# Attention with the mask ahead of the exponentials, row sums on ACT, and a re-planned order of the instructions

## The chip, the cores and the metric

The kernel runs on one core of a Trainium2 chip. The core has five engines with a queue each: PE (matrix multiply), DVE (vector), ACT (activation functions), POOL (GpSimd) and SP, which here only starts DMAs. Each queue is worked off in order, and engines wait for one another by semaphores. Times are device microseconds (us) of one execution; lower is better.

## The reference

One "macaron" layer on x of 8 x 512 tokens with 128 features, in float32: a mixture-of-experts feed-forward, windowed attention, and the same feed-forward again, each added to x. The part that the change touches is the attention:

```
scores = einsum(q, k) / sqrt(128)                 # per window of 128 tokens
_, top_idx = top_k(scores, 32)
masked = where(top 32 of the row, scores, -inf)
attn = softmax(masked - max(masked))
out = attn @ v; out = where(out >= 0, out, 0.01 * out)
x = x + layernorm(out + x_normed) * gamma + beta
```

Each row of 128 scores keeps its 32 largest, and the softmax goes over these alone. The feed-forward normalizes, routes each token to 2 of 8 experts (384 hidden features, SiLU gate times up, then down), weighs the two results, and adds a shared expert of 128 hidden features.

## The kernel before

The 8 batch entries are 8 blocks of 512 tokens; a block is a tile of 128 partitions by 4 windows by 128. Blocks 0 to 3 form group 0, blocks 4 to 7 group 1. The work runs group by group: first feed-forward (norm, routing, experts), attention, second feed-forward. The experts of one group are taken while the attention of the other is under way.

**Routing and experts.** `norm` (from line 532) normalizes a block, writes its rows to DRAM and makes the routing logits, which DVE copies out (`lgs`, line 568). When all four blocks of a group have theirs, `route` (from line 593) sorts the token-expert pairs on DVE, partly with PE; its result `src` (line 742) says which row goes where. Then POOL starts indirect gathers of 128 rows each (`xg`, line 846), PE transposes them (line 858), and 39 tiles of the group go through `pair`: two times three matmuls with the gate and up weights (`pg` and `pu`, line 924), SiLU on ACT (line 932), the product on DVE (`s`, line 935), three matmuls down (`y`, line 940), a copy on ACT (line 954), and an indirect write of the rows by POOL (line 962). The weights of a tile (`wt`) are copied by DVE (line 899) for two of the four runs of experts, and fetched by SP (line 901) for the others. At the end a block's rows are fetched back (`yg`) and added with their gates (line 999).

**Attention** (from line 1037) works on one block at a time: norm, transposes, q, k and v on PE, scores on PE, and a scaled copy of these by ACT into `sc` (line 1074). To find the 32 largest of a row, DVE runs four rounds: `max` gives the 8 largest (line 1084), and `match_replace` writes `tk`, a copy in which they are replaced by TAKEN, -3e38 (line 1088). Each is four instructions, one per window. The first of the maxima, negated, is `nm` (line 1092). `exps` (line 1099) takes exp(sc - max) of all 128 scores of a row on ACT, in place; it needs the first round alone. After the last round one DVE instruction (line 1103) keeps exp where `tk` is TAKEN and puts zero elsewhere. `sums` (lines 1107 and 1108) adds up each row and takes the reciprocal, `rs`. PE transposes the masked values (`pTp`, line 512), ACT copies them out (line 1113), PE multiplies with v (line 1118), and ACT scales each row by `rs` (line 1124). Then follow the leaky step, the residual on POOL, a norm and the sum into x, after which the block goes into the second `norm`.

ACT's Exp and Silu are in different tables; a load (ACT_TABLE_LOAD) comes in front of an activation whose table isn't there.

**The order.** The order of all instructions is worked out when the kernel is built. Each operation is entered in a plan with its engine, an assumed duration, what it reads and writes, and a due time. `schedule` then goes through time: of the operations that can start next on an engine it picks the one that is due first. Due times follow from constants: `PACE` is the spacing of the experts' tiles of the four runs; `LAG` is the spacing of the attention blocks of a group and `STRETCH` how due times grow along a block; `SHARED` sets start and spacing of the shared experts in the first feed-forward; `ROUTE_B` when the first routing of group 1 is due; `PAIRS` and `PUTS` when two parts of the routing are due against the rest; `FINISH` when the last sums of group 0 are due. The queues of SP and POOL are ordered by the same plan. Where the plan sees PE idle for over 0.75 us, it puts in matmuls of an identity whose result (`unread`, line 448) nobody reads; they keep PE busy.

Of the kernel before, what the change touches and what calls it, by code (L numbers as in the profile page):

```python
# [12 lines left out]
AF = mybir.ActivationFunctionType  # L13
ALU = mybir.AluOpType
AX = mybir.AxisListType

P = 128
H = 128
NB = 8
W = 4  # L20
# [7 lines left out]
TAKEN = -3.0e38  # L28
# [30 lines left out]

PACE = (1.79, 2.74, 2.27, 0.89)
LAG, STRETCH, ROUTE_STRETCH = 9.73, -0.34, 3.22
NORM_B, NORM_LAG, NORM_STRETCH = 7.11, 1.83, 1.14
SHARED = ((28.42, 6.74), (33.75, 24.46))
SHARED1 = ((114.02, 8.44), (5.88, 23.46))
ROUTE_B = 38.08
PAIRS, PUTS = 0.5, 4.89
FINISH = 18.87


class Buf:
# [180 lines left out]
def kernel(  # L253
# [16 lines left out]
    nc = tc.nc  # L270
# [32 lines left out]
    def act(us, fn, r, w, **k):  # L303
        return plan.op("ACT", us, fn, r, w, **k)

    def dve(us, fn, r, w, **k):
        return plan.op("DVE", us, fn, r, w, **k)
# [11 lines left out]
    def buf(shape, tag, name, dtype=F32):  # L319
        return Buf(sb, shape, tag, name, dtype)  # L320

    def bank(kind, name):
        return Buf(ps, [P, W, P], "ps", name, kind=f"ps_{kind}")
# [127 lines left out]
    def stats(src, r, name):  # L451

        st, mv = buf([P, W, 6], "st", f"st{name}"), buf([P, W, 2], "mv", f"mv{name}")

        def bn():
            for w in range(W):
                nc.vector.bn_stats(st()[:, w, :], src()[:, w, :])

        def aggr():
            for w in range(W):  # L460
                nc.vector.bn_aggr(mv()[:, w, :], st()[:, w, :])

        dve(0.87, bn, r, [st])
        dve(0.36, aggr, [st], [mv])
        return mv

    def scales(mv, name, eps):

        ve, rstd = buf([P, W], "ve", f"ve{name}"), buf([P, W], "rstd", f"rstd{name}")
        act(0.2, lambda: nc.scalar.activation(ve(), mv()[:, :, 1], AF.Identity, bias=eps),  # L470
            [mv], [ve], hold=[rstd])
        pool(1.05, lambda: nc.gpsimd.tensor_tensor(rstd(), ve(), mhalf, ALU.pow), [ve], [rstd])
        return rstd

    def shifts(mv, rstd, name):
        nb = buf([P, W], "nb", f"nb{name}")
        dve(
            0.16,
            lambda: nc.vector.scalar_tensor_tensor(  # L479
                nb(), mv()[:, :, 0], -1.0, rstd(), ALU.mult, ALU.mult  # L480
            ),
            [mv, rstd], [nb],
        )
        return nb
# [11 lines left out]
    def normalize_act(dst, src, r, rstd, nb):  # L496
        def run():
            for w in range(W):
                nc.scalar.activation(  # L499
                    dst()[:, w, :], src()[:, w, :], AF.Identity,  # L500
                    bias=nb()[:, w : w + 1], scale=rstd()[:, w : w + 1],
                )

        act(1.65, run, [*r, rstd, nb], [dst])
# [532 lines left out]
    def attention(b):  # L1037
        xk = ("x", b)
        ve, mm = nc.vector, nc.tensor.matmul
        h = buf([P, W, H], "h", f"ha_{b}")  # L1040
        mv = stats(lambda: xs[b], [xk], f"_a_{b}")
        rstd = scales(mv, f"_a_{b}", eps1)
        normalize_act(h, lambda: xs[b], [xk], rstd, shifts(mv, rstd, f"_a_{b}"))

        pool(1.27, lambda: nc.gpsimd.tensor_tensor(
            xs[b], xs[b], be_sb.to_broadcast([P, W, H]), ALU.add), [xk, "be"], [xk])
        hT = buf([P, W, P], "a0", f"haT_{b}")
        tp = transposed(h, [h], f"hTp_{b}", hold=[hT])
        act(0.58, lambda tp=tp: nc.scalar.copy(hT(), tp()), [tp], [hT])
        qk = []  # L1050
        for i, c in enumerate("qk"):
            pq, t = bank("m", f"p{c}_{b}"), buf([P, W, P], f"a{i + 1}", f"{c}T_{b}")
            pe(0.85, lambda pq=pq, i=i: mm(pq(), wqkv[:, i, :], hT(), start=True, stop=True),
               [hT, "wqkv"], [pq], hold=[t])
            act(0.68, lambda pq=pq, i=i, t=t: nc.scalar.activation(
                t(), pq(), AF.Identity, bias=bqk_sb[:, i : i + 1]), [pq, "bqk"], [t])
            qk.append(t)
        v, pv = buf([P, W, H], "v", f"v_{b}"), bank("m", f"pv_{b}")

        def values():  # L1060
            for w in range(W):
                mm(pv()[:, w, :], hT()[:, w, :], wqkv[:, 2, :], start=True, stop=True)  # L1062

        pe(0.9, values, [hT, "wqkv"], [pv], hold=[v])
        dve(0.69, lambda: ve.tensor_tensor(v(), pv(), bv_sb.to_broadcast([P, W, H]), ALU.add),
            [pv, "bv"], [v])
        sc, psc = buf([P, W, P], "sc", f"sc_{b}"), bank("m", f"psc_{b}")

        def scores():
            for w in range(W):  # L1070
                mm(psc()[:, w, :], qk[0]()[:, w, :], qk[1]()[:, w, :], start=True, stop=True)

        pe(0.88, scores, qk, [psc], hold=[sc])
        act(0.58, lambda: nc.scalar.activation(sc(), psc(), AF.Copy, scale=float(H) ** -0.5),
            [psc], [sc])

        tk, nm = buf([P, W, P], "a0", f"tk_{b}"), buf([P, W], "nm", f"nm_{b}")
        src = sc
        for r in range(TOPK // 8):
            m8 = buf([P, W, 8], "am8", f"am8_{b}_{r}")  # L1080

            def largest(src=src, m8=m8):
                for w in range(W):
                    ve.max(m8()[:, w, :], src()[:, w, :])

            def take(src=src, m8=m8):
                for w in range(W):
                    ve.match_replace(tk()[:, w, :], m8()[:, w, :], src()[:, w, :], TAKEN)  # L1088

            dve(0.87, largest, [src], [m8])  # L1090
            if r == 0:
                dve(0.17, lambda m8=m8: ve.tensor_scalar(
                    nm(), m8()[:, :, 0], -1.0, None, ALU.mult), [m8], [nm])
            dve(1.08, take, [src, m8], [tk])
            src = tk

        def exps():
            for w in range(W):
                nc.scalar.activation(sc()[:, w, :], sc()[:, w, :], AF.Exp, bias=nm()[:, w : w + 1])

        act(1.3, exps, [sc, nm], [sc], table="exp")
        rs = buf([P, W, 1], "rs", f"rs_{b}")
        dve(0.69, lambda: ve.scalar_tensor_tensor(
            sc(), tk(), TAKEN, sc(), ALU.is_equal, ALU.mult), [tk, sc], [sc])

        def sums():
            ve.tensor_reduce(rs()[:, :, 0], sc(), AX.X, ALU.add)
            ve.reciprocal(rs(), rs())

        dve(0.88, sums, [sc], [rs])  # L1110
        pT = buf([P, W, P], "a1", f"pT_{b}")
        tp = transposed(sc, [sc], f"pTp_{b}", hold=[pT])
        act(0.6, lambda: nc.scalar.copy(pT(), tp()), [tp], [pT])
        po, o = bank("m", f"po_{b}"), buf([P, W, H], "a2", f"o_{b}")

        def mix():
            for w in range(W):
                mm(po()[:, w, :], pT()[:, w, :], v()[:, w, :], start=True, stop=True)

        pe(0.88, mix, [pT, v], [po], hold=[o])  # L1120

        def scaled():
            for w in range(W):
                nc.scalar.activation(o()[:, w, :], po()[:, w, :], AF.Copy, scale=rs()[:, w, :])

        act(1.25, scaled, [po, rs], [o])
        dve(0.68, lambda: ve.scalar_tensor_tensor(o(), o(), NEG_SLOPE, o(), ALU.mult, ALU.max),
            [o], [o])
        pool(1.37, lambda: nc.gpsimd.tensor_tensor(o(), o(), h(), ALU.add), [o, h], [o])
        mv = stats(o, [o], f"_o_{b}")  # L1130
        rstd = scales(mv, f"_o_{b}", eps1)
        normalize_act(o, o, [o], rstd, shifts(mv, rstd, f"_o_{b}"))
        pool(1.27, lambda: nc.gpsimd.tensor_tensor(
            o(), o(), ga_sb.to_broadcast([P, W, H]), ALU.mult), [o, "ga"], [o])
        dve(0.69, lambda: ve.tensor_tensor(xs[b], xs[b], o(), ALU.add), [xk, o], [xk])
# [18 lines left out]
    for g in range(NG):  # L1154
# [4 lines left out]
        for i, b in enumerate(blocks(g)):  # L1159
            at(SHARED[g][0] + i * SHARED[g][1])  # L1160
            shared(0, b)
        at(ROUTE_B * g, 2.0 * g)
        route(0, g)
        at(0.0)
    for g in range(NG):
        experts(0, g, PACE[g])
    for g in range(NG):
# [17 lines left out]
        at(0.0)  # L1185
        experts(1, g, PACE[2 + g])
        diag = {b: weigh(b) for b in blocks(g) if b in LAST_ON_PE}
        for b in sorted(blocks(g), key=lambda b: b % 2):
            if g == 0:
                at(plan.ops[-1].due + FINISH, 2.0)  # L1190
            if b in diag:
# [42 lines left out]
```

## Time and profile before

| | |
|---|---|
| time, median of 3 runs | 530.48 us (529.94 to 531.19) |
| the profiled execution: its time, its span | 636.27 us, 634.6 us |
| granted PE clock, mean | 0.951 |
| PE busy | 532.1 us, 84% |
| DVE busy | 375.4 us, 59% |
| ACT busy | 274.7 us, 43% |
| POOL busy | 368.1 us, 58% |

The profiled execution is one execution, with the recorder on; durations come from it. A row of a group names line, engine, operation, what is written and read, the count, then busy us and mean ns of one, and after the second bar the idle time just ahead of them with what ended it. Busy time of PE is modelled, since matmuls are pipelined. The count of matmul records is twice the count of matmuls here: 156 tiles of three matmuls down are 936 records at line 940.

### The profile page before, as it was taken

How to read it: one execution, taken by the hardware profiler on the slowest of the kernel's cores; microseconds unless marked ns; L12 is line 12 of the kernel's file. 1: busy time of each engine (PE TensorE's matmuls, PEld its weight loads, DVE VectorE, ACT ScalarE, POOL GpSimd, SP SyncE). 2: the span in 40 equal slices, each digit the busy share in tenths (PEclk: the TensorE clock that was granted, in tenths of full speed). 3: DMA queues.
4: the chain of work that ended last, by engine and by line, in shares of the span. 5: the costliest groups of instructions: out<-in, count | busy, mean ns of one | idle time of the engine just before them, and what ended most of it. 6: DMA issues, size and time to landing. Idle time of an engine off the chain costs nothing.

```text
span 634.6 us, 13493 instructions
## 1 busy us (share of the span) xinstructions
PE 532.1 (84%) x4064; PEld 486.0 (77%) x4064; DVE 375.4 (59%) x1440; ACT 274.7 (43%) x588; POOL 368.1 (58%) x484
## 2 busy tenths in 40 slices
PE   4996778796894999989998999899988497679986
PEld 3875767685784978879977889889877387679976
DVE  6485634474330588897479899985685255234412
ACT  5713222221231369887540589886542022223320
POOL 6117454554565477768654788788356446555450
PEclk9998998989998899999999899999999698889999
DMA  7911010111133853445626535366642412111015
GB/s 218 327 61 52 30 38 30 38 31 33 30 109 108 267 156 92 146 140 167 216 89 210 153 116 157 106 183 187 196 151 83 129 58 73 42 34 34 27 38 199
DMA packets 39611, 72.27 MB, mean 114 GB/s; under 512 B 7604, under 2 KB 17848, under 8 KB 39544
## 3 DMA queue, kind: packets, MB, share of 16 engines
q1 hardware_dynamic: 29880, 51.73, 26.5%
q0 software_dynamic: 9088, 18.63, 9.4%
q10 hardware_dynamic: 576, 1.05, 0.4%
q8 instruction: 38, 0.62, 0.4%
q14 instruction: 29, 0.24, 0.1%
HBM read 54.86 MB, written 16.52 MB: 112 GB/s over the span
## 4 chain that ended last, share of the span: by engine, by line
PE 64%; DVE 14%; another core or an unknown queue 8%; ACT 6%; issue 5%; DMA 1%; POOL 1%; DVEq 0%; ACTq 0%
PE y L940 16%; PE pg L924 16%; PE pu L924 14%; DVE s L935 3%; PE ysh L588 2%; PE lg L563 2%; DVE wt L899 2%; PE pus L582 2%; PE xTp L858 2%; PE pgs L579 2%; PE unread L448 2%; ACT n L499 1%; DVE lanes L723 1%; PE pv L1062 1%
## 5 line engine op out<-in xcount | busy, mean ns | idle before, releaser
L962 POOL DMA_INDIRECT ys<-yb,dst x156 | 159.6, 1023 | 157.7 <-ACT yb L954 133.4
L940 PE MATMUL y<-ew,s 128*128 x936 | 140.7, 290 | 59.1 <-DVE s L935 43.5
L940 PEld LDWEIGHTS y<-ew,s 128*128 128x128 f32 x936 | 123.5, 201 | 71.9 <-DVE s L935 36.1
L846 POOL DMA_INDIRECT xg<-rows,src x128 | 126.9, 991 | 70.7 <-issue 34.4
L932 ACT ACTIVATE s<-pg 128x384 f32<-128x384 f32 x156 | 75.4, 490 | 184.6 <-PE pg L924 57.9
L924 PE MATMUL pg<-xT,wt 128*128 (+1 forms) x936 | 138.7, 286 | 13.8 <-issue 10.3
L924 PEld LDWEIGHTS pg<-xT,wt 128*128 128x128 f32 x936 | 123.2, 200 | 22.2 <-issue 17.0
L924 PE MATMUL pu<-xT,wt 128*128 (+1 forms) x936 | 134.6, 281 | 2.0 <-issue 1.0
L899 DVE COPY wt<-egu 128x768 f32 x78 | 45.8, 587 | 135.9 <-PE pu L924 64.0
L924 PEld LDWEIGHTS pu<-xT,wt 128*128 128x128 f32 x936 | 121.9, 198 | 3.2 <-issue 1.5
L935 DVE TENSOR_TENSOR s<-pu,s 128x384 f32<-128x384 f32 x156 | 84.9, 549 | 54.8 <-PE pu L924 19.4
L954 ACT COPY yb<-y 128x512 f32<-128x512 f32 (+1 forms) x60 | 26.0, 435 | 53.5 <-PE y L940 29.7
L999 DVE SCALAR_TENSOR_TENSOR x<-yg,gates,x 128x128 f32<-128x128 f32 x112 | 33.3, 361 | 10.9 <-DMA yg<-ys 10.9
L863 ACT ACTIVATE xT<-xTp,gb 128x512 f32<-128x512 f32 (+2 forms) x34 | 25.5, 754 | 27.3 <-PE xTp L858 19.1
L448 PEld LDWEIGHTS unread<-ident 128*128 128x128 f32 x264 | 31.0, 192 | 1.9 <-issue 1.9
L448 PE MATMUL unread<-ident 128*128 128x128 f32 x264 | 31.8, 275 | 0.0
L563 PEld LDWEIGHTS lg<-rwT,nT 128*128 128x128 f32 x128 | 22.1, 261 | 5.0 <-ACT nT L554 3.1
L1088 DVE MATCH_REPLACE8 tk<-am,tk 128x128 f32<-128x128 f32 x96 | 25.3, 273 | 0.0
L563 PE MATMUL lg<-rwT,nT 128*128 128x8 f32 x128 | 21.9, 302 | 2.9 <-ACT nT L554 2.3
L499 ACT ACTIVATE n<-x,nb,rstd 128x128 f32<-128x128 f32 x56 | 22.8, 484 | 3.3 <-DVE nb L479 3.0
L858 PE MATMUL xTp<-ident,xg 128*128 128x128 f32 x128 | 21.4, 290 | 2.7 <-issue 2.1
L581 ACT ACTIVATE ss<-pgs 128x512 f32<-128x512 f32 x16 | 9.6, 597 | 28.4 <-PE pgs L579 18.8
(177 smaller groups left out, 700.0 us busy)
## 6 DMA issues: line engine op xcount, KB each, us to landing
wt<-in_expert_gu SPq DMA_DIRECT2D x78, 384.0 KB
yg<-ys SPq DMA_DIRECT2D x28, 256.0 KB
rows<-n SPq DMA_DIRECT2D x16, 256.0 KB
egu<-in_expert_gu SPq DMA_DIRECT2D x8, 384.0 KB
ys<-yb,dst POOLq DMA_INDIRECT x156
x<-in_x SPq DMA_DIRECT2D x8, 256.0 KB
xg<-rows,src POOLq DMA_INDIRECT x128
out_x<-x SPq DMA_DIRECT2D x8, 256.0 KB
```

What stands on the lines that cost most here:

```text
L448: plan.idle = lambda: nc.tensor.matmul(unread, ident, ident, start=True, stop=True)
L499: nc.scalar.activation(dst()[:, w, :], src()[:, w, :], AF.Identity, bias=nb()[:, w : w + 1], scale=rstd()[:, w : w + 1],)
L563: nc.tensor.matmul(lg()[:, w, 0:NE], nT()[:, w, :], rwT, start=True, stop=True)
L846: nc.gpsimd.indirect_dma_start(xg()[:, j, :], None, r.rows, bass.IndirectOffsetOnAxis(ap=r.src()[:, t : t + 1], axis=0),)
L858: nc.tensor.transpose(tp()[:, w, :], xg()[:, w, :], ident)
L899: nc.vector.tensor_copy(to, egu[:, bass.ds(row, 2 * FF)])
L924: nc.tensor.matmul(p()[:, f, :], wt()[:, c * NF + f, :], xT[:, bass.ds(offs[1], P)], start=True, stop=True,)
L932: act(0.49, lambda: nc.scalar.activation(s(), pg()[:, 0:NF, :], AF.Silu), [pg], [s], table="silu")
L935: dve(0.56, lambda: nc.vector.tensor_tensor(s(), pu()[:, 0:NF, :], s(), ALU.mult), [pu, s], [s])
L940: nc.tensor.matmul(y()[:, j, :], s()[:, f, :], ew[:, bass.ds(offs[0] + f * H, H)], start=(f == 0), stop=(f == NF - 1),)
L962: ins = nc.gpsimd.indirect_dma_start(r.ys, bass.IndirectOffsetOnAxis(ap=r.dst()[:, t : t + 1], axis=0), yb()[:, i, :], None,).ins
L999: nc.vector.scalar_tensor_tensor(xs[b][:, w, :], yg[k]()[:, w, :], gates()[:, k, q : q + 1], xs[b][:, w, :], ALU.mult, ALU.add,)
```

## The change

In `attention` the mask moves ahead of the exponentials. It is now (tk - TAKEN) - sc: where an element was taken, tk is TAKEN, and the result is -sc; elsewhere it is about 3e38, since the score is lost in the rounding. The exponential takes this with scale -1 and the bias -max, so that a taken element gives exp(sc - max) and the others give 0. Its four instructions each also have ACT write the sum of the row into `rs`. The DVE instruction that added up the rows is gone, and the reciprocal stands alone. Nine constants of the plan have new values, so the whole list of instructions is ordered anew.

```diff
-PACE = (1.79, 2.74, 2.27, 0.89)
-LAG, STRETCH, ROUTE_STRETCH = 9.73, -0.34, 3.22
+PACE = (1.79, 2.74, 2.38, 0.89)
+LAG, STRETCH, ROUTE_STRETCH = 8.76, 0.02, 3.22
 NORM_B, NORM_LAG, NORM_STRETCH = 7.11, 1.83, 1.14
-SHARED = ((28.42, 6.74), (33.75, 24.46))
+SHARED = ((28.42, 4.89), (33.75, 22.74))
 SHARED1 = ((114.02, 8.44), (5.88, 23.46))
-ROUTE_B = 38.08
-PAIRS, PUTS = 0.5, 4.89
-FINISH = 18.87
+ROUTE_B = 33.77
+PAIRS, PUTS = 0.71, 4.31
+FINISH = 13.21
...
+        dve(0.69, lambda: ve.scalar_tensor_tensor(
+            sc(), tk(), TAKEN, sc(), ALU.subtract, ALU.subtract), [tk, sc], [sc])
+        rs = buf([P, W, 1], "rs", f"rs_{b}")
+
         def exps():
             for w in range(W):
-                nc.scalar.activation(sc()[:, w, :], sc()[:, w, :], AF.Exp, bias=nm()[:, w : w + 1])
-
-        act(1.3, exps, [sc, nm], [sc], table="exp")
-        rs = buf([P, W, 1], "rs", f"rs_{b}")
-        dve(0.69, lambda: ve.scalar_tensor_tensor(
-            sc(), tk(), TAKEN, sc(), ALU.is_equal, ALU.mult), [tk, sc], [sc])
-
-        def sums():
-            ve.tensor_reduce(rs()[:, :, 0], sc(), AX.X, ALU.add)
-            ve.reciprocal(rs(), rs())
-
-        dve(0.88, sums, [sc], [rs])
+                nc.scalar.activation(
+                    sc()[:, w, :], sc()[:, w, :], AF.Exp, bias=nm()[:, w : w + 1], scale=-1.0,
+                    accum_out=rs()[:, w, :])
+
+        act(1.3, exps, [sc, nm], [sc, rs], table="exp")
+        dve(0.2, lambda: ve.reciprocal(rs(), rs()), [rs], [rs])
```

The plan's assumed duration of the exponentials stays at 1.3 us; on DVE it books 0.2 us for the reciprocal where it booked 0.88 us for sum and reciprocal.

## The prediction

> **What bounds the kernel now.** I read the page first, then the busy time by stage, the groups of instructions, the chain of work that ended last, and the order of time of each engine around the attention blocks.
>
> ```profile
> span 634.6 us, 13493 instructions
> PE 532.1 (84%) x4064; PEld 486.0 (77%) x4064; DVE 375.4 (59%) x1440; ACT 274.7 (43%) x588; POOL 368.1 (58%) x484
> PE 64%; DVE 14%; another core or an unknown queue 8%; ACT 6%; issue 5%; DMA 1%; POOL 1%; DVEq 0%; ACTq 0%
> ```
>
> PE carries 64% of the chain, so over the whole run it is the bound. The attention blocks are another matter; by stage:
>
> ```profile
> 240.00:280.00 40.00, 35.68 (x286) 32.33 (x285) 36.38 (x184) 35.09 (x75) 30.32 (x31) 1.00 0.45 136
> 320.00:360.00 40.00, 37.23 (x288) 32.24 (x287) 34.52 (x137) 12.53 (x31) 22.01 (x26) 0.96 0.51 159
> 360.00:400.00 40.00, 37.60 (x290) 33.46 (x289) 38.72 (x195) 33.63 (x72) 32.58 (x36) 1.00 0.42 128
> ```
>
> The columns are PE, PEld, DVE, ACT, POOL. In the two attention stages PE, DVE and ACT are all near full: there is no slack engine to push work to. What the stage hands on is seen at its end, in the orders of time of DVE, PE and POOL (start, length, what, idle time before it):
>
> ```profile
> 286.38 0.27 DVE L1088 MATCH_REPLACE8 tk<-am,tk 128x128 f32<-128x128 f32 x1
> 287.25 0.68 DVE L1103 SCALAR_TENSOR_TENSOR sc<-tk,sc 128x512 f32<-128x512 f32 x1
> 315.35 0.19 DVE L568 COPY lgs<-lg 128x32 f32<-128x32 f32 x1 [0.50 <-PE lg L563]
> 339.50 0.19 DVE L742 SCALAR_TENSOR_TENSOR src<-signed 128x32 uint32<-128x32 f32 x1
> 340.36 6.64 PE L448 MATMUL unread<-ident 128*128 128x128 f32 x58
> 344.03 4.87 DMA xg<-rows,src
> 491.26 0.94 PE L924 MATMUL pg<-xT,wt 128*128 x6 [1.20 <-issue]
> ```
>
> Block 3 is the last of its group. From its last match (286.4) its mask, transposes, mix, second norm and logits run one after the other to 315.35; routing follows to 339.5, POOL's first gathers land at 348.9, and only then do the experts of the next group start. Meanwhile PE has run out of experts' tiles: it multiplies identities that nobody reads, 29 of them or 6.6 us at 340 alone. So the end of block 3, and not PE, sets when PE gets work again. The same happens to block 7, more mildly: PE does such fillers from 485.9, and real work starts at 491.26.
>
> **Profiled and timed.** The profiled execution took 636.27 us (span 634.6), 106 us over the median of 530.48. The chain books 8.2% of the span, 52 us, on an unknown queue and 4.7%, 30 us, on issue, and after long pauses three expert matmuls take 1.28 us instead of 0.67. These pauses lie mostly in the expert-only stages; I found none over 2 us in 222 to 315. So I take the attention rows as they stand and carry the difference to the median microsecond for microsecond: a sum of +x means 636.27+x there and 530.48+x timed.
>
> **The change, part by part.** The rows it touches:
>
> ```profile
> L1099 ACT ACT_TABLE_LOAD x8 | 10.3, 1283 | 0.5 <-DVE tk L1088 0.3
> L1099 ACT ACTIVATE sc<-sc,nm 128x128 f32<-128x128 f32 x32 | 10.2, 390 | 0.1
> L1103 DVE SCALAR_TENSOR_TENSOR sc<-tk,sc 128x512 f32<-128x512 f32 x8 | 6.3, 789 | 0.0
> L1107 DVE TENSOR_REDUCE rs<-sc 128x4 f32<-128x512 f32 x8 | 5.3, 665 | 0.0
> L1108 DVE RECIPROCAL rs<-rs 128x4 f32<-128x4 f32 x8 | 1.4, 178 | 0.3
> L639 ACT ACTIVATE th<-th 128x16 f32<-128x16 f32 x4 | 0.8, 212 | 2.6 <-DVE th L638 2.6
> ```
>
> *Removed.* Eight row sums L1107 on DVE, 8 x 0.665 = 5.3 us of DVE in all. On the path to block 3's end lie at most those of blocks 0, 1 and 2 (its own comes behind its mask): 3 x 0.67 = 2.0 us if DVE were the bound throughout. It isn't: between the takes DVE stands idle 1.55 us at 251 and 1.65 us at 264, waiting for PE, and the chain runs over DVE only from 266 to 284, with one L1107 in it. So the gain is 0.67 to 2.0; I take 1.3.
>
> *Same instructions.* The mask stays one instruction of two inputs and the same size: 0.68 for 0.68. Its maximum of 1.58 us was one case beside POOL's addition at 243.2, which other neighbours could repeat or spare: -0.9 to +0.9, taken as 0. Scaling by -1 costs nothing, since the activation has its scale anyway. The reciprocal keeps its 0.18.
>
> *Moved.* Today the exponentials of a block need only the first take; ACT does them while DVE runs the three other rounds (block 3: load at 278.64, exponentials 279.94 to 281.2, mask at 287.25). Afterwards they need the mask, which needs the last take. That cover, some 6 us of DVE work, is gone, and the transposes of the probabilities wait for ACT instead of DVE. On the path come 4 exponentials, 1.28 us as a group (four of 0.39 that overlap), and the table load in front of them, 1.28 us, since the load itself waited on DVE in one of eight cases and would do so always when placed behind the wait. One more hand-over between engines: 0.1 us, from gaps of 0.02 to 0.3. If the exponentials of two blocks become neighbours, or the load is issued ahead, 1.28 goes away; so the term is 1.4 to 2.7, and I take 2.7. The step issues no DMA and passes nothing on SP's or POOL's queue.
>
> Here the Trainium skill speaks against the change more strongly: "ScalarE: Activation LUTs", section "What ACT_TABLE_LOAD costs", books 1.28 us for the load and another 1.38 us of draining for each switch. The row shows 1283 ns, and at 278.64 the exponentials begin 1.30 us after the load does, with the load itself 0.02 us behind its predecessor. By the rule block 3 would pay 4.0 instead of 2.7; I go by the row.
>
> *Added.* ACT's sums: no row shows an activation with such an output. The skill's "VectorE: DVE Perf Modes", section "Two Vector instructions with no wait between them", says that on DVE such an instruction is two, the second one reading the accumulator; if ACT does likewise, four reads a block follow. Bounds: nothing, or 4 x 0.21 (the smallest ACT row, L639) = 0.85 us a block, 6.8 us of ACT in all. I take 0.2 each, 0.8 a block, nearer to that row than to nothing, because the sum of each partition has to be written out by something.
>
> *A new wait.* The reciprocal on DVE now waits for ACT, where it followed DVE's own sum. Behind it in DVE's queue stand the next block's takes and the products L935, on which PE's y waits. If the list expects the exponentials 0.8 us early, DVE loses up to that in each of eight blocks, 3 of them ahead of a group's last. I take 0.2 on the path, bounds 0 and 2.4.
>
> *The order.* Later blocks of attention come due earlier (LAG 9.73 to 8.76: 1, 1.9 and 2.9 us for the second to fourth), so PE prefers them to tiles more often. At most the 3.2 us that DVE waited for PE come back, at worst as much is lost elsewhere, since all other due times of shared experts, routing and combining move too and with them SP's weight loads and POOL's gathers and puts: -2.9 to +2.9. I take -0.7, about one matmul group of 0.67 that a later block no longer waits for.
>
> *Sum on block 3's path:* 2.7 + 0.8 + 0.2 - 1.3 - 0.7 = +1.7 us. It lands in full, because it lengthens a stretch in which PE does fillers. For block 7 the same terms hold. The two don't add: attention of the second group starts from the writes of the first experts, which end about 331, and not from the routing of block 3; so the last experts start about 1.7 us later, once. The timed forecast is 530.48 + 1.7 = 532.2, in the profiled execution's own terms 638.0.
>
> **The rivals.** *Faster: DVE's relief and the order win.* If DVE is the bound throughout, all 2.0 come back, and if the order returns 2.9 while the table load leaves the path: 1.4 + 0.8 - 2.0 - 2.9 = -2.7, or 527.8. For it: DVE at 38.72 of 40 us. Against it: DVE waits for PE between takes, and block 3's end is a chain with no room. It decides from the point where block 3's logits come earlier than 28.9 us behind its last match plus what DVE gained. *Slower by more: ACT becomes the bound.* ACT is at 35.09 of 40 us; 0.8 a block in a full queue and exponentials queued behind other blocks' norms (1.65 us) give 2.7 + 0.8 + 1.65 + 1.5 for the DVE wait - 1.3 = +5.4, or 535.9. *No change to be measured:* PE fills the longer chain with tiles that the order kept back, or the accumulator is free and relief full: 2.7 - 2.0 - 0.7 = 0, or 530.5.
>
> **How the numbers follow.** A measurement here tells about 0.2%, 1.1 us, from no change. Likeliest case (531.6 to 534.5) 0.42; ACT as the bound 0.20; no change 0.11; faster 0.27. This gives slower 0.62, same 0.11, faster 0.27. The range reaches from 526.0, a little below the faster rival, for bounds of the order, to 537.5, for bounds of the waits.
>
> **What the new profile would show.** L1107 gone and about 0.67 less DVE per block; the exponentials behind the last match, with an ACT table load between mask and exponentials; from block 3's last match to its logits 32 us instead of 28.9; small ACT instructions of some 0.2 us between the exponentials; longer fillers ahead of the second routing's gathers. The prediction is wrong if that stretch has no fillers any more, if the order starts block 3 over 3 us sooner, or if the opening stage (PE fillers at 37 to 43), whose due times change too, moves by itself.

## The result, and the profile after

The changed kernel takes 536.13 us (median of 5 runs, 535.89 to 538.61); the kernel before, 530.77 us beside it (529.94 to 532.55). The ratio is 1.0114, 95% interval 1.0083 to 1.0146: slower, by 5.4 us. The forecast was 532.2 with a range of 526.0 to 537.5, and slower was the likeliest outcome at 0.62. So direction and range hold. The size does not: +1.7 was forecast, and the time is that of the rival in which ACT becomes the bound (535.9). In the experiments further down the runs of one kernel spread by up to 3%; times there are medians of all runs, while ratios and their intervals compare the fast runs alone (within 1.5% of the fastest), so that the two need not agree.

From the page of the changed kernel: the span, busy time of the engines, and the chain by engine.

```profile
span 536.9 us, 13595 instructions
PE 505.5 (94%) x4106; PEld 469.9 (88%) x4106; DVE 370.2 (69%) x1432; ACT 278.8 (52%) x620; POOL 369.9 (69%) x486
PE 62%; DVE 11%; ACT 9%; DMA 9%; POOL 3%; issue 3%; SPq 1%; ACTq 0%; DVEq 0%; POOLq 0%
```

DVE's busy time fell by 5.2 us, as the removed row sums say; ACT's rose by 4.1. ACT's share of the chain went from 6% to 9%, and DVE's from 14% to 11%. This execution took 538.61 us, the slowest of the five, 0.5% over the median. The profile of before had 636.27; its "unknown queue" of 8% is absent here. More on that below.

Busy time in 40 us of group 0's attention (PE, PEld, DVE, ACT, POOL):

```profile
200.00:240.00 40.00, 38.33 (x301) 34.57 (x300) 33.16 (x171) 38.41 (x97) 30.87 (x34) 1.00 0.50 154
```

Before, ACT had 35.09 of 40 us there, and DVE 36.38. The two have changed places: ACT 38.41, DVE 33.16. The windows are not the same work to the instruction, so this is a hint only.

The groups of instructions that the change touches:

```profile
L1104 ACT ACTIVATE sc<-sc,nm 128x128 f32<-128x128 f32 x32 | 12.4, 390 | 0.1
L1104 ACT ACT_TABLE_LOAD x8 | 10.3, 1283 | 0.1
L1104 ACT ACTIVATION_READ_ACCUMULATOR sc<-sc,nm 128x1 f32 x32 | 6.0, 187 | 0.0
L1109 DVE RECIPROCAL rs<-rs 128x4 f32<-128x4 f32 x8 | 1.3, 162 | 0.6 <-ACT sc L1104 0.6
L448 PE MATMUL unread<-ident 128*128 128x128 f32 x306 | 36.5, 275 | 0.0
```

The accumulator is indeed an instruction of its own on ACT, 187 ns. Table loads are 8, as before. PE does 153 fillers (306 records) where it did 132 (264 records, 31.8 us in all): the 42 added records are all of PE's 42 more (4106 for 4064). The orders of time of DVE, ACT and PE around block 3, the last of group 0, and up to the second routing:

```profile
228.08 0.27 DVE L1088 MATCH_REPLACE8 tk<-am,tk 128x128 f32<-128x128 f32 x1
229.58 0.68 DVE L1098 SCALAR_TENSOR_TENSOR sc<-tk,sc 128x512 f32<-128x512 f32 x1
229.93 1.64 ACT L499 ACTIVATE n<-x,nb,rstd 128x128 f32<-128x128 f32 x4
231.47 0.28 ACT L470 ACTIVATE ve_o<-mv_o,eps 128x4 f32<-128x4 f32 x1
231.77 1.28 ACT L1104 ACT_TABLE_LOAD   x1
233.07 0.40 ACT L1104 ACTIVATE sc<-sc,nm 128x128 f32<-128x128 f32 x1
...
234.62 0.76 ACT L554 ACTIVATE nT<-nTp,gb 128x512 f32<-128x512 f32 x1
235.29 1.64 ACT L499 ACTIVATE o<-o,nb_o,rstd_o 128x128 f32<-128x128 f32 x4
236.82 0.57 ACT L1112 COPY pT<-pTp 128x512 f32<-128x512 f32 x1
...
237.89 1.28 ACT L932 ACT_TABLE_LOAD   x1
...
239.57 1.14 ACT L1123 ACTIVATE o<-po,rs 128x128 f32<-128x128 f32 x4
...
261.80 0.19 DVE L568 COPY lgs<-lg 128x32 f32<-128x32 f32 x1 [0.84 <-PE lg L563]
...
279.57 3.51 PE L448 MATMUL unread<-ident 128*128 128x128 f32 x30
...
284.25 8.51 PE L448 MATMUL unread<-ident 128*128 128x128 f32 x74
```

And the same two steps of ACT in the kernel before (its mask ran 287.25 to 287.93):

```profile
289.37 0.58 ACT L1113 COPY pT<-pTp 128x512 f32<-128x512 f32 x1
291.30 1.14 ACT L1124 ACTIVATE o<-po,rs 128x128 f32<-128x128 f32 x4 [0.36 <-PE po L1118]
```

From the last match to the scaling of the output it is 11.49 us now (228.08 to 239.57), and was 4.92 (286.38 to 291.30). The difference of 6.57 splits, step by step, into: mask begun later behind the match, 1.50 for 0.87, +0.63; exponentials after the mask's end, +2.81, of which 1.51 stand behind another block's norm and `ve_o` and 1.30 behind the table load; the exponentials with their reads, 233.07 to 234.72, +1.65; from there to the copy of the probabilities 2.10 for 1.44, +0.66; from the copy to the scaling 2.75 for 1.93, +0.82. The copy waits for nothing that PE does: PE's four transposes began at 234.47 and took 0.63. It stands in ACT's queue behind `nT` and a norm. The scaling likewise stands behind a copy, Silu's table load and a Silu. By the logits, 1.8 us of the 6.57 are made up: last match to logits is 33.7 us for 29.0, where 32 had been forecast.

Block 7, the last of group 1, pays more. Its last match and the scaling of its output, first now, then before:

```profile
358.64 0.27 DVE L1088 MATCH_REPLACE8 tk<-am,tk 128x128 f32<-128x128 f32 x1
371.65 1.12 ACT L1123 ACTIVATE o<-po,rs 128x128 f32<-128x128 f32 x4
416.15 0.27 DVE L1088 MATCH_REPLACE8 tk<-am,tk 128x128 f32<-128x128 f32 x1
421.26 1.14 ACT L1124 ACTIVATE o<-po,rs 128x128 f32<-128x128 f32 x4 [0.65 <-PE po L1118]
```

That is 13.01 us for 5.11, and up to the logits 37.3 (395.96) for 31.1 (447.22): +6.2, against +4.7 at block 3.

The fillers tell what idle time of PE the plan foresaw while it waits for the second routings and their gathers. The kernel before has, behind block 3, the 58 records at 340.36 and two batches ahead of them; behind block 7 it has 6, 8 and 6 from 485.88 on:

```profile
334.16 2.84 PE L448 MATMUL unread<-ident 128*128 128x128 f32 x24
337.88 0.69 PE L448 MATMUL unread<-ident 128*128 128x128 f32 x4
487.89 1.06 PE L448 MATMUL unread<-ident 128*128 128x128 f32 x8
```

The changed kernel has the 30 and 74 shown above behind block 3, and 22, 18 and 6 from 425.80 on behind block 7:

```profile
425.80 2.62 PE L448 MATMUL unread<-ident 128*128 128x128 f32 x22
429.18 2.17 PE L448 MATMUL unread<-ident 128*128 128x128 f32 x18
```

So behind block 3 fillers went from 43 to 52 (10.2 to 12.0 us, +1.9), behind block 7 from 10 to 23 (2.7 to 5.6 us, +2.9). Their number is set by the list, whatever the chip; it is no measured wait.

The chain of work that ended last, in order of time (start, length, what), in the attention of group 0 and at block 7:

```profile
201.05 1.28 ACT L1104
202.34 1.65 ACT sc L1104 x8
...
206.02 1.27 ACT L932
...
214.56 1.58 ACT sc L1104 x8
...
217.36 1.28 ACT L932
...
231.77 1.28 ACT L1104
233.07 1.65 ACT sc L1104 x8
...
361.93 1.28 ACT L1104
...
363.54 1.34 ACT sc L1104 x7
...
365.75 1.28 ACT L932
```

The pieces at L1104 alone are the load of the exponentials' table, `sc` with them the exponentials, and those at L932 alone the load of Silu's table that has to follow. The chain runs through the exponentials of blocks 1, 2 and 3, and again of block 7. In group 0 these lines add up to 10.0 us (two loads, three sets of exponentials, two loads back). In the chain of the kernel before, the same stretch holds no exponential at all and one table load; of the moved work only a mask is in it:

```profile
242.84 1.28 ACT L932
272.32 0.59 DVE sc L1103
```

In group 1 the chain of the kernel before does hold exponentials with their loads, those of blocks 4 and 6:

```profile
368.25 1.28 ACT L1099
369.55 1.28 ACT sc L1099 x4
...
393.51 1.28 ACT L1099
...
395.11 0.97 ACT sc L1099 x3
```

So in group 0 the exponentials are new on the chain; in group 1 they moved on it, from blocks 4 and 6 to block 7, and the chain alone shows no growth there. Behind block 3's exponentials the chain goes on over PE's queue of experts (from 237.45), as it did before (from 284.43). The tail and PE's own work end close to each other: DVE is done with the counts for the routing at 275.1, and PE's queue comes to their matmuls (`rank`, line 664) at 275.84; before, it was 328.1 and 329.26.

### The profile page after: what moved, and what is told of

The parts are those of the page before. It is cut to its first block, busy times and chain, and to the rows that moved or that the text cites. A ratio compares the mean times of both kernels' runs of the same rounds, so it can differ in the third digit from the quotient of the medians.

```text
span 536.9 us, 13595 instructions
## 1 busy us (share of the span) xinstructions
PE 505.5 (94%) x4106; PEld 469.9 (88%) x4106; DVE 370.2 (69%) x1432; ACT 278.8 (52%) x620; POOL 369.9 (69%) x486
## 4 chain that ended last, share of the span: by engine, by line
PE 62%; DVE 11%; ACT 9%; DMA 9%; POOL 3%; issue 3%; SPq 1%; ACTq 0%; DVEq 0%; POOLq 0%
PE pg L924 16%; PE pu L924 15%; PE y L940 15%; DMA xg<-rows,src 3%; DVE tk L1088 3%; PE pgs L579 3%; DVE am L1084 2%; DMA wt<-in_expert_gu 2%; PE lg L563 2%; PE pus L582 2%; PE ysh L588 2%; PE xTp L858 2%; ACT n L499 2%; POOL xg L846 2%; DMA ys<-yb,dst 1%
## 5 line engine op out<-in xcount | busy, mean ns | idle before, releaser
L846 POOL DMA_INDIRECT xg<-rows,src x128 | 128.4, 1003 | 71.8 <-issue 32.1
L924 PE MATMUL pg<-xT,wt 128*128 (+1 forms) x936 | 133.2, 279 | 8.3 <-DMA wt<-in_expert_gu 2.5
L932 ACT ACTIVATE s<-pg 128x384 f32<-128x384 f32 x156 | 76.2, 491 | 113.1 <-PE pg L924 108.6
L924 PEld LDWEIGHTS pg<-xT,wt 128*128 128x128 f32 x936 | 118.5, 193 | 16.3 <-issue 8.2
L940 PE MATMUL y<-ew,s 128*128 x936 | 130.4, 276 | 1.7 <-ACT yb L954 1.0
L924 PE MATMUL pu<-xT,wt 128*128 (+1 forms) x936 | 131.4, 277 | 0.0
L940 PEld LDWEIGHTS y<-ew,s 128*128 128x128 f32 x936 | 117.1, 192 | 6.4 <-issue 3.2
L924 PEld LDWEIGHTS pu<-xT,wt 128*128 128x128 f32 x936 | 117.7, 193 | 0.7 <-issue 0.5
L899 DVE COPY wt<-egu 128x768 f32 x78 | 44.6, 571 | 57.0 <-PE pu L924 56.0
L448 PEld LDWEIGHTS unread<-ident 128*128 128x128 f32 x306 | 35.7, 192 | 2.0 <-issue 2.0
L448 PE MATMUL unread<-ident 128*128 128x128 f32 x306 | 36.5, 275 | 0.0
```

What stands on the lines that cost most here:

```text
L448: plan.idle = lambda: nc.tensor.matmul(unread, ident, ident, start=True, stop=True)
L846: nc.gpsimd.indirect_dma_start(xg()[:, j, :], None, r.rows, bass.IndirectOffsetOnAxis(ap=r.src()[:, t : t + 1], axis=0),)
L899: nc.vector.tensor_copy(to, egu[:, bass.ds(row, 2 * FF)])
L924: nc.tensor.matmul(p()[:, f, :], wt()[:, c * NF + f, :], xT[:, bass.ds(offs[1], P)], start=True, stop=True,)
L932: act(0.49, lambda: nc.scalar.activation(s(), pg()[:, 0:NF, :], AF.Silu), [pg], [s], table="silu")
L940: nc.tensor.matmul(y()[:, j, :], s()[:, f, :], ew[:, bass.ds(offs[0] + f * H, H)], start=(f == 0), stop=(f == NF - 1),)
```

## The experiments

The theory (A): behind the mask, the exponentials come onto the path that sets a group's end; this costs more than DVE's relief returns, and the new list of instructions wins part of it back. Rivals: (B) the sums on ACT are what costs; (C) the new list itself is the loss and the edit is harmless; (D) DVE's relief is worth far more or less than 1.3 us.

On the chips of these runs the kernel before itself takes 644 to 663 us. In its three profiles PE, DVE and ACT stand still together for up to 8 us at a time, in gaps over 0.3 us 44 to 51 us in all (4 us in the profile of the changed kernel above), and the mean granted clock of its runs is 0.92 to 0.96 (0.996 to 0.999 in the five runs of the changed kernel above); the rest of the difference was not looked into. Ratios are therefore taken on one chip alone, and stages against a trace of before from the same chip. "Stage" below is the time from the first maximum of a group's first block to the logits of its last. In three traces of before from these chips it is 84.9, 87.0 and 83.7 us for group 0 (83.6 in the profile shown before) and 82.2, 88.9 and 83.0 for group 1 (81.6).

**The kernel before, once on each of three chips**, for its traces.

> The kernel before, unchanged, for a second profiled execution, since the first one was 106 us longer than the timed runs. Both theories: about 530.5 us; if the pauses of the first profile belong to that execution alone, the span now is near 529 us, and the attention rows are as in the first profile: 28.9 us from block 3's last match to its logits. If the pauses belong to the kernel, the span is again well over 600 us.

> The kernel before, unchanged, once more. If its pauses depend on the chip that it runs on, about 530.5 us and a span near 529 with no pause over 2 us; if they come with any profile, again some 640 us. Attention rows as in the first two profiles: about 29 us from block 3's last match to its logits, 84 to 85 us from block 0's first maxima to block 3's logits.

> The kernel before, for a profile beside the kernel after on the same chip. Where the chip shows the pauses of the first profile, 640 to 670 us; where it doesn't, about 530.5 us, and then from block 0's first maxima to block 3's logits 82 to 84 us.

Measured in that one profiled execution: 644.73, 667.32 and 647.83 us. Block 3's tail, last match to logits, is 29.2, 29.6 and 29.0 us against 29.0 in the profile before, so this stretch lies outside the pauses. Block 7's is 31.3, 35.5 and 31.0 us against 31.1. In the third trace such a pause ends at 565.54: PE waits 4.22 us for DVE, which in turn stands 6.17 us on something that the profile can't name, and the first three matmuls afterwards take twice as long (1.65 us for 0.83).

**The edit alone, in the list of before** (every other instruction stays where it was):

```diff
-                nc.scalar.activation(sc()[:, w, :], sc()[:, w, :], AF.Exp, bias=nm()[:, w : w + 1])
+                nc.scalar.activation(
+                    sc()[:, w, :], sc()[:, w, :], AF.Exp, bias=nm()[:, w : w + 1], scale=-1.0,
+                    accum_out=rs()[:, w, :])
...
-        act(1.3, exps, [sc, nm], [sc], table="exp")
-        dve(0.69, lambda: ve.scalar_tensor_tensor(
-            sc(), tk(), TAKEN, sc(), ALU.is_equal, ALU.mult), [tk, sc], [sc])
+        act(1.3, lambda: None, [sc, nm], [sc], table="exp")
...
+        def mask():
+            ve.scalar_tensor_tensor(sc(), tk(), TAKEN, sc(), ALU.subtract, ALU.subtract)
+            exps()
...
-        dve(0.88, sums, [sc], [rs])
+        dve(0.69, mask, [tk, sc], [sc])
+        dve(0.88, lambda: ve.reciprocal(rs(), rs()), [sc], [rs])
```

The plan still sees the exponentials where they were, but nothing is issued there; they are issued behind the mask.

> The instructions of the kernel after, placed in the list of the kernel before: exponentials with their sums right behind the mask, the reciprocal where sum and reciprocal stood, every other instruction in its old place. Theory A (the exponentials on the path of blocks 3 and 7 are the cause): 533 to 537 us, with 3 to 4 us more from block 3's last match to its logits. Theory B (the new order is the cause, the edit itself costs nothing or gains): 529 to 531 us.

Measured: 665.17 against 647.95 us, ratio 1.0392 [1.0235, 1.0549]; theory A's 533 to 537 us would be 1.004 to 1.012, so it is far too low. The stages are 92.7 and 94.4 us, +7.8 and +12.2 on the same chip's trace of before. The group of the reciprocals in this kernel:

```profile
L1112 DVE RECIPROCAL rs<-rs 128x4 f32<-128x4 f32 x8 | 1.4, 178 | 13.1 <-ACT sc L1101 13.1
```

And its order of time of ACT at block 3, where the mask runs from 293.74 to 294.42:

```profile
291.83 1.28 ACT L1101 ACT_TABLE_LOAD   x1
294.46 0.40 ACT L1101 ACTIVATE sc<-sc,nm 128x128 f32<-128x128 f32 x1 [1.34 <-DVE sc L1108]
...
297.67 1.28 ACT L932 ACT_TABLE_LOAD   x1
...
299.35 0.58 ACT L1115 COPY pT<-pTp 128x512 f32<-128x512 f32 x1
```

The tail of block 3 is 32.7 us, +3.5, as theory A had it; that of block 7 is 37.3, +6.0. The rest of group 0's +7.8 arises ahead of block 3's tail; the wait of the reciprocal, 13.1 us over eight blocks, stops all of DVE behind it and fits that. And the table load is issued ahead of the wait: here it is over before the mask begins, and the exponentials start as the mask ends. In its place Silu's load now stands between them and the copy of the probabilities. So in this list the edit is not harmless. The list was not made for it, though: the total holds what its stopped queues cost, and is no price of the edit in a list of its own.

**The instructions of before, in the list of after** (exponentials issued right behind the first take, sum back on DVE ahead of the reciprocal):

```diff
-            dve(1.08, take, [src, m8], [tk])
+            if r == 0:
+                def take_and_exps(take=take):
+                    take()
+                    for w in range(W):
+                        nc.scalar.activation(
+                            sc()[:, w, :], sc()[:, w, :], AF.Exp, bias=nm()[:, w : w + 1])
+
+                dve(1.08, take_and_exps, [src, m8], [tk])
+            else:
+                dve(1.08, take, [src, m8], [tk])
...
+        act(1.3, lambda: None, [sc, nm], [sc, rs], table="exp")
...
-        dve(0.88, sums, [sc], [rs])
+        dve(0.2, sums, [rs], [rs])
```

> The reverse: the list of the kernel after, but with exponentials behind the first take, the mask behind the last one and the row sum on DVE, as in the kernel before. Theory A: 2 to 4 us faster than the kernel after, so 532 to 534 us. Theory B: as slow as the kernel after, 535.5 to 537 us.

Measured: 673.35 us, ratio 1.0504 [1.0399, 1.0609]; stages 90.8 and 101.9 us. This is slower than either kernel, and neither theory had it. Its line of ACT's groups shows a cost that no theory named:

```profile
L1098 ACT ACT_TABLE_LOAD x8 | 10.3, 1283 | 6.7 <-DVE tk L1088 5.6 <-DVE am L1084 1.0
```

ACT stands for 6.7 us at the place that the list hadn't meant for exponentials, with all else queued behind. So this run says nothing for or against the exponentials' place: an instruction put into another's list costs by where it stops a queue.

**The sums back on DVE, all else as in the changed kernel**, run twice; the second time beside the changed kernel itself:

```diff
-                    sc()[:, w, :], sc()[:, w, :], AF.Exp, bias=nm()[:, w : w + 1], scale=-1.0,
-                    accum_out=rs()[:, w, :])
+                    sc()[:, w, :], sc()[:, w, :], AF.Exp, bias=nm()[:, w : w + 1], scale=-1.0)
...
-        dve(0.2, lambda: ve.reciprocal(rs(), rs()), [rs], [rs])
+        dve(0.2, sums, [rs], [rs])
```

> The kernel after in its own list, with the row sums on DVE again (a reduce ahead of the reciprocal) and none on ACT. ACT is relieved of 8 x 0.37 us, DVE takes on 8 x 0.67. If ACT's sums are a large part of the loss: 533 to 534.5 us. If the relief of DVE is worth something: 537 to 539 us. Theory A, in which the place of the exponentials is the cause: within 1 us of 536.1.

> The changed kernel again, beside the next one on the same chip, so that the accumulator reads of ACT can be priced apart from all else. Theory (the exponentials behind the mask cost, the sums hardly): ratio to before 1.01 to 1.025 as in the two comparisons so far. Four exponentials with their reads at a pitch of 1.65 us, last match to logits of the first group 33.5 to 34.

> The changed kernel with the row sums taken by DVE again, list unchanged. If the 32 accumulator reads of ACT cost what they show (0.37 us for each block's four, partly on the path), this one is up to 1 us faster in each group of four blocks, against 1.3 us given back for the sums on DVE: equal to the changed kernel within 0.5%. Rival, the reads are what made the change slow: 4 us or more below the changed kernel on this chip. Other rival, DVE's relief was worth more than the 1.4 us a group found so far: over 4 us above it.

Measured: 666.86 us, ratio 1.0304 [1.0116, 1.0492]; then, on one chip, 664.54 us for the changed kernel, 1.0233 [1.0143, 1.0323], and 666.74 for this one, 1.0307 [1.0216, 1.0399]. The two don't differ by more than their intervals. Group 0's stage is 88.9 us with the sums on DVE and 87.4 with them on ACT; group 1's is 95.5 and 99.2, so the stages point both ways. The order of time of ACT at block 3, sums on DVE:

```profile
297.59 1.28 ACT L1104 ACTIVATE sc<-sc,nm 128x128 f32<-128x128 f32 x4
...
300.97 0.57 ACT L1116 COPY pT<-pTp 128x512 f32<-128x512 f32 x1
```

Without the reads four exponentials take 1.28 us, with them 1.65: the reads cost 0.37 a block, not 0.8. The copy still comes 2.1 us behind the exponentials, for want of its turn. B falls as the main cause: without the reads the kernel is no faster.

**DVE's relief alone** (the kernel before, leaving out its row sum: rows are not divided by their sums, the reciprocal is taken of `nm`):

```diff
-        dve(0.88, sums, [sc], [rs])
+        dve(0.88, lambda: ve.reciprocal(rs()[:, :, 0], nm()), [sc], [rs])
```

> The kernel before in its own list, with DVE's row sum left out and nothing in its place (the reciprocal is taken of the maxima instead, so rows are not divided by their sums). This is DVE's relief alone. If DVE bounds the attention stages: 2 to 4 us faster than before, 526.5 to 528.5. If the relief is worth next to nothing, because DVE waits for PE and ACT in the list anyway: 529.5 to 530.8 us.

Measured: 660.52 against 662.75 us, ratio 0.9924 [0.9876, 0.9972]. Stages 85.6 and 87.5 us, against 87.0 and 88.9 on the same chip: 1.4 us in each group. D falls, the forecast had 1.3. The whole gain by the ratio is 5.0 us [1.9, 8.2], more than the 1.4 that it would be if it counted once; but the medians of all runs differ by 2.2 us only, so that it counts in both groups is likely and not shown.

**The new code with the old constants, and the old code with the new ones** (each ordered anew by the plan), the latter beside the changed kernel on a third chip:

The first takes the part of the diff in `attention` and none of the constants, against the kernel before:

```diff
-        act(1.3, exps, [sc, nm], [sc], table="exp")
...
-        dve(0.88, sums, [sc], [rs])
+        act(1.3, exps, [sc, nm], [sc, rs], table="exp")
+        dve(0.2, lambda: ve.reciprocal(rs(), rs()), [rs], [rs])
```

The second takes the constants alone:

```diff
-PACE = (1.79, 2.74, 2.27, 0.89)
-LAG, STRETCH, ROUTE_STRETCH = 9.73, -0.34, 3.22
+PACE = (1.79, 2.74, 2.38, 0.89)
+LAG, STRETCH, ROUTE_STRETCH = 8.76, 0.02, 3.22
...
-ROUTE_B = 38.08
+ROUTE_B = 33.77
```

> The code of the kernel after with the nine old constants, planned anew. Theory A (the exponentials behind the mask cost time, and new constants win some of it back): slower than the kernel after, 537 to 546 us. Theory B (the new constants are the loss): 529 to 532 us.

> The kernel after, unchanged, beside the kernel before on this chip. Theory A (a longer tail of each group's last block, part of it won back by the order): 1.008 to 1.015 of the kernel before where there are no pauses; where there are, the same 5 us and what pauses happen to add, 1.00 to 1.04.

> The code of the kernel before with the nine new constants, planned anew: exponentials early, row sums on DVE. Theory A: the constants suit the longer chain only, so on the old code they lose something, 1.005 to 1.02 of the kernel before. Theory B (the new constants are the loss, whatever the code): as slow as the kernel after or slower. If the constants are better in themselves: below 1.000.

Measured: new code with old constants 677.7 us, ratio 1.0213 [1.0126, 1.03]; the changed kernel 662.4 us, 1.0238 [1.0153, 1.0323]; old code with new constants 657.21 us, 1.0209 [1.0114, 1.0303]. Stages in the order of these runs: group 0 89.6 (before on this chip 87.0), 86.6 and 90.0 (before 83.7); group 1 100.7 (before 88.9), 98.7 and 87.0 (before 83.0). So the new constants are a loss for the old code (+6.2 and +4.0 us in the stages), and for the new code they are neither a gain nor a loss that shows (1.0213 with the old, 1.0233 and 1.0238 with the new ones). The list as such matters too: the new code in the old list costs 1.0392 and ordered anew, by either set, about 1.02; these intervals overlap, so that is likely and not proven.

C is not excluded. The old code with the new constants (1.0209) is as slow as the changed kernel beside it (1.0238), as theory B had forecast for this run. With the old constants the edit costs 2.1%; with the new ones no price of its own can be told from none. What these runs do tell apart is where the time goes: the old code with the new constants loses in both groups' stages (+6.2 and +4.0), the changed kernel little in group 0's (+2.5 on one chip and +2.9 on the other) and most in group 1's. There it is 99.2 us for 82.2 on one chip and 98.7 for 83.0 on the other, +17.0 and +15.7. The stage of group 1 of the first pair, before and changed (length, then busy time of PE, PEld, DVE, ACT, POOL):

```profile
369.51:451.75 82.24, 79.09 (x631) 73.37 (x629) 66.50 (x323) 66.29 (x144) 67.31 (x78) 0.98 0.51 154
373.27:472.51 99.24, 89.99 (x704) 81.51 (x702) 68.82 (x330) 74.35 (x174) 73.14 (x87) 0.98 0.48 146
```

Part of it is work and no loss: PE takes 73 more records of matmuls in the stage. Part is block 7's tail, 44.3 and 43.9 us there for 31.3 and 31.0. Why that tail is longer than the 37.3 us of the first profile stays open.

The same runs warn of a reading. Block 3's tail is 34.4 us in the old code with the new constants, as long as the 34.0 of the changed kernel on that chip, though its exponentials run early: an order alone can lengthen the tail. In the changed kernel block 3's last match comes 2.0 and 2.3 us sooner after the group's first maximum than in the kernel before on the same chips (52.7 for 54.7, 53.4 for 55.7), which returns that much of the tail's +4.9 and +4.8. So the tail prices the edit only where the list is the same (+3.5); elsewhere the whole stage has to be taken.

## Why the prediction was right in direction and wrong in size

- **The bound.** Right in the main: PE does fillers behind the end of block 3, though the chain itself goes over PE's queue there, about 1 us behind the tail. The forecast that they grow held: from 43 (10.2 us) to 52 (12.0 us), +1.9 us, near the +1.7 forecast for this path.
- **Exponentials and table load on the path, 2.7; ACT's sums, 0.8; DVE's wait, 0.2.** Together 3.7 us, and in the same list block 3's tail grew by 3.5. The sum is near, its make-up is not. The load is not held back by the wait: it ran ahead where ACT was free (edit in the old list), and lay on the path where ACT came late (changed kernel). The reads cost 0.37. In their place, work of other blocks in ACT's queue, a load of Silu's table among it, came between mask, exponentials, copy and scaling. The reciprocal waits 0.6 us in all in the changed kernel, as small as taken, but 13.1 where the list was not made for it.
- **DVE's relief, -1.3.** Right: 1.4 in each group's stage.
- **The order, -0.7.** No gain shows from the new constants. What ordering anew as such returns looks larger in group 0's stage, from +7.8 us to +2.5 to +2.9 (changed kernel against before on two chips); in group 1's it goes the other way, from +12.2 to +15.7 and +17.0.
- **"Sum on block 3's path ... The two don't add ... once."** This is the step that failed. The price was worked out for block 3 and counted once, and block 7 was taken to pay the same and to add nothing. In the run that kept the list of before, both groups paid (+7.8 and +12.2), and the two profiled executions, 660.74 and 644.73 us, differ by 16.0: more than either group. In the changed kernel block 7's tail grew more than block 3's (+6.2 for +4.7), and the fillers grew in both places. An estimate from these fillers: 1.9 us behind block 3 and 2.9 behind block 7, 4.8 together, of the 5.4 measured. It is an estimate only, since fillers are what the plan foresaw: the new code with the old constants has 195 of them (46.6 us) at about the same ratio.
- **"So I take the attention rows as they stand and carry the difference ... microsecond for microsecond."** Wrong for a chip with pauses: there the change costs 15 us (1.0233 of 646.5 and 1.0238 of 644.5), and 5.4 where the kernel takes 530. The tail rows of block 3 did stand, at 29.0 to 29.6 us; the total did not carry, and most of it arises in group 1's stage (+15.7 and +17.0).
- **The rival that hit.** "ACT becomes the bound" gave +5.4 for 2.7 + 0.8 + 1.65 + 1.5 - 1.3. Its mechanism is the one that group 0's chain shows, and its wait behind other blocks' norms was 1.51 at block 3 (1.65 taken). But 0.8 was 0.37, and DVE's wait of 1.5 did not come. That the total agrees is largely luck: it left out the second group as well.

Still open: how the 5.4 us divide between the edit and the new order, as the old code with the new constants was as slow, and neither it nor the edit alone ran on a chip without pauses; and how they divide between the groups, beyond the estimate from the fillers, as there is no trace of the kernel before from such a chip. Group 0's first part (first maximum to block 3's last match) is 48.3 us in the profile after and 53.4 for the same kernel on a chip with pauses, so most of the 6.3 us that it seems to have gained on the profile before (54.7) goes with the chip; for the same reason its stage of 82.05 us can't be set against the 83.6 of before, nor 86.45 against 81.6 without reserve. What makes the pauses was not found.

## What to carry to other kernels

When a step is moved behind the last result of a block, price its place in the receiving engine's queue, not its duration alone: look at how full that engine is in this very stage (ACT had 35 of 40 us here) and what stands in the queue between the step and each of its successors. Count the price for every block whose path it enters, in every group, before deciding that it lands once. And put new code into the old list for one run: with the list held fixed, single waits show what the edit does. The total of such a run is no price, since a step in a list that was not made for it also stops a queue (13.1 us on DVE here, and 6.7 us on ACT in the reverse). To tell an edit from the order that came with it, run the old code under the new constants too.

## What was not expected of the hardware

- An activation that also gives the row's sum is followed by an instruction of its own, ACTIVATION_READ_ACCUMULATOR, 187 ns. Four pairs take 1.65 us and four plain exponentials 1.28: the read adds 0.09 us each.
- A table load can be issued ahead of what its activation waits for. At 291.83, with the edit in the old list, it began 2.6 us ahead of the exponentials, which then waited for DVE. It need not be: in the reverse run the loads themselves waited for DVE, 6.7 us over eight.
- The same kernel takes 530 us in one set of runs and 644 to 663 on three chips of the later ones. In their profiles PE, DVE and ACT stand still together for up to 8 us at a time, nearly always outside the two attention stages.
